# Seven block products in place of eight in a float32 feed-forward stage

## Chip, cores and metric

The kernel runs on one core of a Trainium2 chip. The metric is the device time of one execution in microseconds (us); lower is better. "Before" is the kernel as it was, "after" the changed one. A profiled execution gives a page (busy times, the chain of work that ended last, groups of instructions) and a trace that can be asked for single stretches of time. Engines are PE (TensorE), DVE (VectorE), ACT (ScalarE), POOL (GpSimd) and SP, which issues most DMAs.

## What is computed

A decoder of two layers, float32 throughout, for 8 sequences of 112 tokens and width 512: self-attention, cross-attention and feed-forward in each layer, each added to x. The change is in the last of them, layer 1's feed-forward, which works on the LayerNorm of x:

```python
def _L1_ffn_ref(x, w_gate, w_up, w_down):      # DIM_IN 512, DIM_HIDDEN 2048
    gate = jnp.einsum('bsd,hd->bsh', x, w_gate)
    up = jnp.einsum('bsd,hd->bsh', x, w_up)
    gated = jax.nn.silu(gate) * up
    return jnp.einsum('bsh,dh->bsd', gated, w_down)
...
x = x + _L1_ffn_ref(_layernorm(x, axis=-1), L1_ffn_w_gate, L1_ffn_w_up, L1_ffn_w_down)
```

## The kernel before

**Sizes.** There are NT = 896 tokens in NTT = 7 tiles of P = 128; HALF = 448 is half of the tokens, KC = 4 the number of blocks of 128 in the width of 512, NI = 256. x lies in SBUF as seven tiles `x[t]` of 128 tokens by 512.

**Stages.** The kernel runs one stage after another in one program. The changed stage, `l1_feed_forward` (line 1864), is the last. Before it, `l1_cross_attention` ends with a conditional part and, behind it, the output projections of the last two tiles (`project_out` on tiles 5 and 6, lines 1697 to 1701). After it, line 1891 stores the seven tiles of x, with one DMA of 256 KB each on SP's queue, in the order of tiles.

**The stage.** `layernorm_T` (line 247) normalises the seven tiles (VectorE, ScalarE for the root), transposes them on TensorE (line 235) and copies them on ScalarE (line 239) to `hT`, which holds the normalised tokens with the width on the partitions: 4 blocks of 128 by 896 tokens. The 2048 hidden units are 16 blocks of 128, in four weight tiles each of gate and up (`load_w`, line 155: 1 MB, four blocks of the width by 512 hidden units). For each block and each half of the tokens `gated` (line 1383) makes two products of four terms with `matmul_k` (line 257, its matmul at line 259), one into a bank of `mm_ps` and one into a bank of `sc_ps`: the weight block of 128x128 is stationary, 448 tokens move. ScalarE takes Silu of the gate's bank (line 1391), VectorE multiplies it by the up's bank (line 1392) into `h`, 16 blocks by 896 tokens. Then for each tile of tokens one product of 16 terms, with 128 tokens of `h` stationary and 512 columns of `wd` moving, goes into a bank of `tp_ps` (line 1878), and VectorE adds it to `x[t]` (line 1880).

**Buffers.** PSUM is eight banks of 128x512 float32 (`bank`, line 111), named by hand: `mm_ps` takes 0 and 1 in turn, `sc_ps` 2 and 3, `tp_ps` 4 and 5. The weight tiles rotate through the six buffers of the pool `wp` (line 94), so the load of the third down tile, for example, waits until the third gate tile has been read. A pool opened later takes SBUF that an earlier one has given back, and its first writes wait for the earlier one's last reads.

**Order.** In this stage no order is pinned by hand. When the program is built, each engine gets one queue, filled in the order in which the code is written, but work that is written later can be let ahead of work that is not yet ready. Within its queue an engine takes instructions strictly in turn. Semaphores are added where one engine needs another's result, or a buffer back.

A float32 matmul appears in the trace as two records of TensorE, each with its own weight load.

Of the kernel before, what the change touches and what calls it, by code (L numbers as in the profile page):

```python
# [21 lines left out]
FP = mybir.dt.float32  # L22
# [3 lines left out]
AF = mybir.ActivationFunctionType  # L26
ALU = mybir.AluOpType
# [3 lines left out]
P = 128  # L31
# [3 lines left out]
NTT = NT // P  # L35
HALF = NT // 2
# [6 lines left out]
NEXP, NI, TOPK = 32, 256, 8  # L43
# [15 lines left out]
def decoder(ctx: ExitStack, tc: tile.TileContext, a, out: bass.AP):  # L59
# [24 lines left out]
    V, A, G, T = (Engine(e) for e in (nc.vector, nc.scalar, nc.gpsimd, nc.tensor))  # L84
# [9 lines left out]
    wp = ctx.enter_context(tc.tile_pool(name="wp", bufs=6))  # L94
# [3 lines left out]
    work = [None]  # L98
    ps = ctx.enter_context(tc.tile_pool(name="ps", bufs=2, space=PSUM))

    @contextmanager
    def phase(name, waits="pool"):

        with tc.tile_pool(name=name, bufs=1, reuse_waits=waits) as stay, tc.tile_pool(
            name=f"{name}w", bufs=2, reuse_waits=waits
        ) as w:
            work[0] = w
            yield stay


    bank = [ps.tile([P, 512], FP, tag=f"bank{i}", name=f"bank{i}", bufs=1) for i in range(8)]
    turns = {"mm": 0, "sc": 0, "tp": 0}

    def turn(what):
        turns[what] += 1
        return turns[what] % 2

    def mm_ps():
        return bank[turn("mm")]

    def sc_ps():
        return bank[2 + turn("sc")]

    def tp_ps():
        return bank[4 + turn("tp")]
# [25 lines left out]
    x = [xp.tile([P, D], FP, tag=f"x{t}", name=f"x{t}") for t in range(NTT)]  # L151
# [3 lines left out]
    def load_w(src, name):  # L155
        w = wp.tile([P, 4, 512], FP, tag="w", name=name)
        nc.sync.dma_start(w, src)
        return w
# [88 lines left out]
    def layernorm_T(hT, root=rsqrt):  # L247
        for t in range(NTT):
            mvr = row_scales(x[t], root)
            xn = normed_rows()  # L250
            normed(xn, x[t], mvr)
            transpose_tile(hT, xn, t)

    def new_hT():
        return act.tile([P, KC, NT], FP, tag="hT", name="hT")

    def matmul_k(dst, lhs, rhs, n=KC):
        for k in range(n):
            T.matmul(dst, lhs(k), rhs(k), start=(k == 0), stop=(k == n - 1))  # L259
# [140 lines left out]
    def all_of(pieces):  # L400

        while True:
            try:
                next(pieces)
            except StopIteration as end:
                return end.value
# [106 lines left out]
    def any_early():  # L513

        with tc.tile_pool(name="early", bufs=1) as tmp:
            return counted_early(tmp)
# [863 lines left out]
                V.tensor_tensor(x[t], x[t], odd[:, t, :], ALU.add)  # L1380
            sort.close()

    def gated(dst, wg, wu, hT, halves=(0, 1)):

        for half in halves:
            tok = slice(half * HALF, (half + 1) * HALF)
            pg, pu = mm_ps(), sc_ps()
            matmul_k(pg[:, :HALF], lambda k: wg[:, k, :], lambda k: hT[:, k, tok])
            matmul_k(pu[:, :HALF], lambda k: wu[:, k, :], lambda k: hT[:, k, tok])
            sg = work[0].tile([P, HALF], FP, tag="sg", name="sg")  # L1390
            A.activation(sg, pg[:, :HALF], AF.Silu)
            V.tensor_tensor(dst[:, tok], sg, pu[:, :HALF], ALU.mult)  # L1392


    def l1_self_attention():
# [466 lines left out]


    def l1_feed_forward():
        with phase("f1") as p0:
            hT = new_hT()
            layernorm_T(hT)
            h = p0.tile([P, 16, NT], FP, tag="hid", name="hid")
            for i in range(4):
                wg, wu = load_w(a["f1_wg"][i], "f1_wg"), load_w(a["f1_wu"][i], "f1_wu")  # L1870
                for c in range(4):
                    cs = slice(c * P, (c + 1) * P)
                    gated(h[:, 4 * i + c, :], wg[:, :, cs], wu[:, :, cs], hT)
            wd = [load_w(a["f1_wd"][i], "f1_wd") for i in range(4)]
            for t in range(NTT):
                po = tp_ps()
                matmul_k(
                    po, lambda k: h[:, k, t * P : (t + 1) * P], lambda k: wd[k // 4][:, k % 4, :], 16
                )
                V.tensor_tensor(x[t], x[t], po, ALU.add)  # L1880

    early0, early1 = any_early()
    l0_self_attention()
    with tc.tile_pool(name="y", bufs=1) as yp:
        y_all = yp.tile([P, NTT, D], FP, tag="y", name="y")
        y = [y_all[:, t, :] for t in range(NTT)]
        l0_block(yp, y, *l0_cross_attention(early0, y))
    l1_cross_attention(early1, l1_self_attention())
    l1_feed_forward()
    for t in range(NTT):  # L1890
        nc.sync.dma_start(out[t * P : (t + 1) * P, :], x[t])
# [106 lines left out]
```

## Time and profile before

| what | us |
|---|---|
| median of 3 runs (lowest, highest) | 2064.79 (2064.42, 2069.33) |
| profiled execution, its time | 2061.26 |
| profiled execution, its span (first to last instruction) | 2059.5 |
| TensorE busy in the span | 1960.6 |
| first product of the changed stage starts at | 1765.10 |
| last product of the ups ends, products with `wd` begin at | 1959.2 |
| last add to x starts at | 2055.53 |
| mean granted TensorE clock over the span | 0.978 |

Times inside the profile count from the span's start. In the lists below, a line of the timeline reads: start, length, engine, line of the kernel, operation, what is written from what, shape, number of records merged, and in brackets how long the engine stood idle before and who released it. A group's line ends with busy time, the mean of one, idle time before its instructions and the releaser. A line of the chain has start, length, engine, tile and line. Line L80 is that of the helper that issues instructions where an order is pinned, so many operations of earlier stages share it. Records of matmuls overlap: the length of one is not the distance between two.

### The profile page before, as it was taken

The numbers are of one execution on the slowest core, as the hardware profiler recorded it, in microseconds if no ns is written. First come the engines' busy times: TensorE is split into PE (matmuls) and PEld (weight loads), VectorE is DVE, ScalarE is ACT, GpSimd is POOL, SyncE is SP. The second block draws the span as 40 slices with busy tenths as digits, with TensorE's granted clock in tenths as the row PEclk, the third lists the DMA queues.
The fourth block names the chain that finished last, engine by engine and source line by source line (L and its number), as shares of the span: only waits on it lengthen the run. The fifth ranks groups of instructions, "written<-read, shape, count | busy, mean of one in ns | idle before, by whom it ended". The sixth has DMA issues, their size and how long they took to land. (4 is left out here: it accounts for less than half of the span.)

```text
span 2059.5 us, 26414 instructions
## 1 busy us (share of the span) xinstructions
PE 1960.6 (95%) x10033; PEld 1172.4 (57%) x10033; DVE 905.4 (44%) x1929; ACT 561.7 (27%) x1316; POOL 609.0 (30%) x766
## 2 busy tenths in 40 slices
PE   8999989999999999988999999988899898999999
PEld 4545664455555555555778888854556454455544
DVE  4662556375666656645222222233776465310100
ACT  3543321021222212332111111121666465200000
POOL 2252032132222222222566666612554122000000
PEclk9999989999999999989999999999999999999999
DMA  4105010243334433446877677660011301011100
GB/s 175 42 22 171 13 42 32 77 143 116 133 125 134 148 115 120 155 146 249 244 188 187 159 180 183 129 166 24 22 37 36 94 22 63 22 41 41 41 16 21
DMA packets 82021, 209.62 MB, mean 102 GB/s; under 512 B 32979, under 2 KB 38227, under 8 KB 72788
## 3 DMA queue, kind: packets, MB, share of 16 engines
q1 hardware_dynamic: 57588, 134.27, 19.7%
q0 software_dynamic: 24288, 73.47, 14.0%
q8 instruction: 85, 1.39, 0.3%
q14 instruction: 60, 0.49, 0.1%
HBM read 245.31 MB, written 78.76 MB: 157 GB/s over the span
## 5 line engine op out<-in xcount | busy, mean ns | idle before, releaser
L259 PE MATMUL bank<-f_wo,oT 128*128 128x512 f32 x448 | 210.5, 594 | 0.0
L259 PE MATMUL bank<-hT,f_wq 128*128 128x448 f32 x512 | 202.6, 540 | 0.0
L80 PEld LDWEIGHTS bank<-hbT,wb 128*128 128x128 f32 x1408 | 164.0, 192 | 20.2 <-issue 20.2
L80 PE MATMUL bank<-hbT,wb 128*128 128x128 f32 x1408 | 164.3, 275 | 0.0
L80 DVE TENSOR_TENSOR hidb<-sgb,bank 128x256 f32<-128x256 f32 x66 | 27.8, 421 | 289.5 <-ACT sgb L80 289.5
L904 POOL TENSOR_TENSOR s<-s,rec 112x448 f32<-112x448 f32 x64 | 59.7, 933 | 322.3 <-ACT pT L306 258.2
L259 PEld LDWEIGHTS bank<-hT,f_wq 128*128 128x128 f32 x512 | 93.8, 190 | 78.2 <-issue 78.0
L80 POOL TENSOR_TENSOR st<-st,rec 112x448 f32<-112x448 f32 (+1 forms) x95 | 82.8, 903 | 146.0 <-DVE rec L80 80.9
L259 PEld LDWEIGHTS bank<-f_wo,oT 128*128 128x128 f32 x448 | 80.7, 190 | 76.0 <-issue 76.0
L80 POOL DMA_INDIRECT acc<-ob,row_out x66 | 106.3, 1610 | 35.2 <-issue 18.3
L80 ACT ACTIVATE st<-st,mxs 112x112 f32<-112x112 f32 (+1 forms) x383 | 111.0, 380 | 0.0
L298 ACT ACTIVATE s<-s 112x448 f32<-112x448 f32 x64 | 36.9, 577 | 243.9 <-DVE s L297 229.3
L259 PE MATMUL bank<-hT,f_wg 128*128 128x448 f32 x256 | 101.9, 539 | 0.0
L259 PE MATMUL bank<-hT,f_wu 128*128 128x448 f32 x256 | 101.4, 539 | 0.0
L259 PE MATMUL bank<-f_wd,hid 128*128 128x512 f32 x224 | 96.3, 592 | 0.0
L1392 DVE TENSOR_TENSOR hid<-sg,bank 128x448 f32<-128x448 f32 x32 | 19.9, 621 | 172.7 <-PE bank L259 172.7
L922 DVE TENSOR_TENSOR y<-y,bank 128x512 f32<-128x512 f32 x56 | 38.5, 687 | 124.6 <-PE bank L259 124.6
L848 POOL TENSOR_TENSOR qT<-qT,qs 128x448 f32<-128x448 f32 x64 | 72.3, 1130 | 63.4 <-DVE qs L844 63.4
L844 DVE TENSOR_TENSOR qs<-bank,shape_consts 64x448 f32<-64x448 f32 x144 | 89.5, 622 | 2.9
L80 PE MATMUL bank<-wb,hidb 128*128 128x512 f32 x176 | 84.0, 600 | 0.0
L80 ACT ACTIVATE sgb<-bank 128x256 f32<-128x256 f32 x66 | 25.4, 384 | 196.8 <-PE bank L80 196.8
L80 ACT ACTIVATE ob<-bank,pw 128x512 f32<-128x512 f32 x66 | 45.4, 687 | 122.3 <-PE bank L80 122.3
(363 smaller groups left out, 3417.3 us busy)
## 6 DMA issues: line engine op xcount, KB each, us to landing
weights<-in_e_wg SPq DMA_DIRECT2D x64, 256.0 KB
weights<-in_e_wu SPq DMA_DIRECT2D x64, 256.0 KB
weights<-in_e_wd SPq DMA_DIRECT2D x64, 256.0 KB
f_wq<-in_f_wq SPq DMA_DIRECT2D x8, 1024.0 KB
f_wo<-in_f_wo SPq DMA_DIRECT2D x8, 1024.0 KB
cTe<-in_ctxT SPq DMA_DIRECT2D x8, 558.0 KB
f_wg<-in_f_wg SPq DMA_DIRECT2D x4, 1024.0 KB
f_wu<-in_f_wu SPq DMA_DIRECT2D x4, 1024.0 KB
```

Source lines behind the costliest of these rows:

```text
L80: done = issue(*args, **kw)
L259: T.matmul(dst, lhs(k), rhs(k), start=(k == 0), stop=(k == n - 1))
L298: A.activation(s, s, AF.Exp)
L844: V.tensor_tensor(qs[lo : lo + 64], src[hi : hi + 64], sin0[lo : lo + 64].unsqueeze(1).to_broadcast([64, HB, S]), ALU.mult,)
L848: G.tensor_tensor(d, d, qs, ALU.add)
L904: G.tensor_tensor(s, s, rec.unsqueeze(2).to_broadcast([S, 4, S]), ALU.mult)
L922: V.tensor_tensor(y[t], y[t], project_rows(oT, wo, t), ALU.add)
L1392: V.tensor_tensor(dst[:, tok], sg, pu[:, :HALF], ALU.mult)
```

## The change

The two matrix products of the stage (tokens by gate and up weights, hidden units by down weights) are each cut into 2x2 blocks and computed with seven block products in the Strassen-Winograd form instead of eight.

For gates and ups, two hidden blocks of 128 are the rows, two halves of the width the inner index and two halves of the tokens the columns. Four sums of weight blocks (`row_sums`, on GpSimd, for each weight and each pair of hidden blocks) and four sums of token blocks (`column_sums`, on VectorE, once) are formed first. For the down product, two tiles of tokens are the rows, even and odd blocks of the hidden units the inner index, and two halves of 256 columns of `wd` the columns: four column sums of 128x8x256 on VectorE once, four row sums of 128x8x128 on GpSimd for each of three pairs of tiles. The seventh tile is computed as before, ahead of the pairs, into bank 6.

`seven_products` uses three banks a, b and c. Four products accumulate in a, and ScalarE copies a out after the first, the second and the third; two go into c, and VectorE reads c between them; one goes into b. Each of the four results is a bank's content plus, in three cases, one of the copies: for gates VectorE adds and ScalarE takes Silu, for ups VectorE adds and GpSimd multiplies (the fourth is multiplied on VectorE from the bank), for the down product GpSimd adds the copy to x and VectorE adds the bank. Gates use banks 0 to 2 and ups 3 to 5, as do even and odd pairs of tiles. `in_turn` interleaves the groups: first product of a group, then the rest of the group before it, then the middle of the group.

```diff
-    def gated(dst, wg, wu, hT, halves=(0, 1)):
-        for half in halves:
-            tok = slice(half * HALF, (half + 1) * HALF)
-            pg, pu = mm_ps(), sc_ps()
-            matmul_k(pg[:, :HALF], lambda k: wg[:, k, :], lambda k: hT[:, k, tok])
-            matmul_k(pu[:, :HALF], lambda k: wu[:, k, :], lambda k: hT[:, k, tok])
-            sg = work[0].tile([P, HALF], FP, tag="sg", name="sg")
-            A.activation(sg, pg[:, :HALF], AF.Silu)
-            V.tensor_tensor(dst[:, tok], sg, pu[:, :HALF], ALU.mult)
+    def row_sums(dst, top, bottom, eng):
+        eng.tensor_tensor(dst(0), bottom[0], bottom[1], ALU.add)
+        eng.tensor_tensor(dst(1), dst(0), top[0], ALU.subtract)
+        eng.tensor_tensor(dst(2), top[0], bottom[0], ALU.subtract)
+        eng.tensor_tensor(dst(3), top[1], dst(1), ALU.subtract)
+
+    def column_sums(dst, left, right, eng):
+        eng.tensor_tensor(dst(0), right[0], left[0], ALU.subtract)
+        eng.tensor_tensor(dst(1), right[1], dst(0), ALU.subtract)
+        eng.tensor_tensor(dst(2), right[1], right[0], ALU.subtract)
+        eng.tensor_tensor(dst(3), left[1], dst(1), ALU.subtract)
+
+    def seven_products(banks, n, terms, top, bottom, rows, left, right, columns, copies, take):
+        a, b, c = (bank[:, :n] for bank in banks)
+
+        def product(dst, lhs, rhs, first=False, part=None):
+            for k in range(terms) if part is None else part:
+                T.matmul(dst, lhs(k), rhs(k), start=first and k == 0, stop=k == terms - 1,
+                         skip_group_check=True)
+
+        def copied(i):
+            A.copy(copies[i], a)
+            return copies[i]
+
+        few = range(terms if terms < 4 else terms // 2)
+        product(a, top[0], left[0], first=True)
+        m1 = copied(0)
+        yield
+        product(c, rows[0], columns[0], first=True)
+        product(a, rows[1], columns[1])
+        u2 = copied(1)
+        product(b, top[1], left[1], first=True, part=few)
+        product(a, rows[2], columns[2])
+        u3 = copied(2)
+        yield
+        take(1, 1, c, u3)
+        product(b, top[1], left[1], part=range(len(few), terms))
+        take(0, 0, b, m1)
+        product(a, bottom[1], columns[3])
+        take(1, 0, a, None)
+        product(c, rows[3], right[1])
+        take(0, 1, c, u2)
+
+    def in_turn(products):
+        last = iter(())
+        for one in products:
+            next(one)
+            all_of(last)
+            next(one)
+            last = one
+        all_of(last)
...
     def l1_feed_forward():
...
-            for i in range(4):
-                wg, wu = load_w(a["f1_wg"][i], "f1_wg"), load_w(a["f1_wu"][i], "f1_wu")
-                for c in range(4):
-                    cs = slice(c * P, (c + 1) * P)
-                    gated(h[:, 4 * i + c, :], wg[:, :, cs], wu[:, :, cs], hT)
...
+                tokens = [gp.tile([P, 2, HALF], FP, tag=f"tok{i}", name=f"tok{i}") for i in range(4)]
+                for kk in range(2):
+                    column_sums(lambda i: tokens[i][:, kk, :],
+                                *([of_hT(k, half)(kk) for k in range(2)] for half in range(2)), V)
+
+                def projected(w, p, banks, take):
...
+                    sums = gp.tile([P, 4, 2, P], FP, tag="sums", name="sums", bufs=3)
+                    row_sums(lambda i: sums[:, i], *([block(m, k) for k in range(2)] for m in range(2)),
+                             G)
+                    copies = [gp.tile([P, HALF], FP, tag=f"copy{i}", name="copy", bufs=2)
+                              for i in range(3)]
+                    return seven_products(
+                        banks, HALF, 2, *([of(block(m, k)) for k in range(2)] for m in range(2)),
+                        [of(sums[:, i]) for i in range(4)],
+                        *([of_hT(k, half) for k in range(2)] for half in range(2)),
+                        [of(t) for t in tokens], copies, take,
+                    )
+
+                def gates_and_ups(wg, wu, p, dst):
+                    gates = {}
+
+                    def take_gate(m, half, pp, more):
+                        g = gates[m, half] = gp.tile([P, HALF], FP, tag="g", name="g", bufs=7)
+                        if more is not None:
+                            V.tensor_tensor(g, pp, more, ALU.add)
+                            pp = g
+                        A.activation(g, pp, AF.Silu)
+
+                    def take_up(m, half, pp, more):
+                        d = dst[:, m, half * HALF : (half + 1) * HALF]
+                        g = gates[m, half]
+                        if more is None:
+                            V.tensor_tensor(d, pp, g, ALU.mult)
+                        else:
+                            V.tensor_tensor(more, pp, more, ALU.add)
+                            G.tensor_tensor(d, more, g, ALU.mult)
+
+                    yield projected(wg, p, (bank[0], bank[1], bank[2]), take_gate)
+                    yield projected(wu, p, (bank[3], bank[4], bank[5]), take_up)
+
+                def all_gates_and_ups():
+                    for i in range(4):
+                        wg, wu = load_w(a["f1_wg"][i], "f1_wg"), load_w(a["f1_wu"][i], "f1_wu")
+                        for p in range(2):
+                            c = 4 * i + 2 * p
+                            yield from gates_and_ups(wg, wu, p, h[:, c : c + 2])
+
+                in_turn(all_gates_and_ups())
             wd = [load_w(a["f1_wd"][i], "f1_wd") for i in range(4)]
-            for t in range(NTT):
-                po = tp_ps()
-                matmul_k(
-                    po, lambda k: h[:, k, t * P : (t + 1) * P], lambda k: wd[k // 4][:, k % 4, :], 16
-                )
...
+                columns = [wp.tile([P, 8, NI], FP, tag="w", name="colsum") if i < 2 else
+                           dp.tile([P, 8, NI], FP, tag=f"colsum{i}", name="colsum") for i in range(4)]
+                for i in range(4):
+                    column_sums(lambda m: columns[m][:, 2 * i : 2 * i + 2],
+                                columns_of(i, 0), columns_of(i, 1), V)
+
+                t = NTT - 1
+                po = bank[6]
+                matmul_k(po, lambda k: h[:, k, t * P : (t + 1) * P],
+                         lambda k: wd[k // 4][:, k % 4, :], 16)
                 V.tensor_tensor(x[t], x[t], po, ALU.add)
+
+                def two_tiles(p):
+                    top, bottom = rows_of(2 * p), rows_of(2 * p + 1)
+                    rows = [dp.tile([P, 8, P], FP, tag=f"rowsum{i}", name="rowsum", bufs=2)
+                            for i in range(4)]
+                    row_sums(lambda i: rows[i], top, bottom, G)
+                    copies = [dp.tile([P, NI], FP, tag=f"ucopy{i}", name="ucopy", bufs=2)
+                              for i in range(3)]
+
+                    def take(m, n, pp, more):
+                        d = x[2 * p + m][:, n * NI : (n + 1) * NI]
+                        if more is not None:
+                            G.tensor_tensor(d, d, more, ALU.add)
+                        V.tensor_tensor(d, d, pp, ALU.add)
+
+                    return seven_products(
+                        bank[:3] if p % 2 == 0 else bank[3:6], NI, 8,
+                        [of(r) for r in top], [of(r) for r in bottom], [of(r) for r in rows],
+                        *([columns_by(k, n) for k in range(2)] for n in range(2)),
+                        [of(c) for c in columns], copies, take,
+                    )
+
+                in_turn(two_tiles(p) for p in range(NTT // 2))
```

More of the change, by code (lines that the diff above doesn't have):

```diff
@@ L1868, in l1_feed_forward, with of_hT @@
             h = p0.tile([P, 16, NT], FP, tag="hid", name="hid")
-            for i in range(4):
-                wg, wu = load_w(a["f1_wg"][i], "f1_wg"), load_w(a["f1_wu"][i], "f1_wu")
-                for c in range(4):
-                    cs = slice(c * P, (c + 1) * P)
-                    gated(h[:, 4 * i + c, :], wg[:, :, cs], wu[:, :, cs], hT)
-            wd = [load_w(a["f1_wd"][i], "f1_wd") for i in range(4)]
-            for t in range(NTT):
-                po = tp_ps()
-                matmul_k(
-                    po, lambda k: h[:, k, t * P : (t + 1) * P], lambda k: wd[k // 4][:, k % 4, :], 16
-                )
-                V.tensor_tensor(x[t], x[t], po, ALU.add)
+            def of_hT(k, half):
+                return lambda kk: hT[:, 2 * k + kk, half * HALF : (half + 1) * HALF]
@@ new lines, in of, with block @@
+            def of(block):
+                return lambda kk: block[:, kk, :]
+            with ExitStack() as pools:
+                gp = pools.enter_context(tc.tile_pool(name="gates", bufs=1))
+                tokens = [gp.tile([P, 2, HALF], FP, tag=f"tok{i}", name=f"tok{i}") for i in range(4)]
[3 more added lines that the diff above has]
+                def projected(w, p, banks, take):
+                    def block(m, k):
+                        c = (2 * p + m) * P
+                        return w[:, 2 * k : 2 * k + 2, c : c + P]
+                    sums = gp.tile([P, 4, 2, P], FP, tag="sums", name="sums", bufs=3)
[34 more added lines that the diff above has]
+                in_turn(all_gates_and_ups())
@@ new lines, in l1_feed_forward, with rows_of, columns_of, columns_by @@
+            wd = [load_w(a["f1_wd"][i], "f1_wd") for i in range(4)]
+            def rows_of(t):
+                return [h[:, k::2, t * P : (t + 1) * P] for k in range(2)]
+            def columns_of(i, n):
+                return [wd[i][:, k::2, n * NI : (n + 1) * NI] for k in range(2)]
+            def columns_by(k, n):
+                return lambda kk: wd[kk // 2][:, 2 * (kk % 2) + k, n * NI : (n + 1) * NI]
+            with tc.tile_pool(name="down", bufs=1) as dp:
+                columns = [wp.tile([P, 8, NI], FP, tag="w", name="colsum") if i < 2 else
[7 more added lines that the diff above has]
+                         lambda k: wd[k // 4][:, k % 4, :], 16)
+                V.tensor_tensor(x[t], x[t], po, ALU.add)
+                def two_tiles(p):
[17 more added lines that the diff above has]
+                in_turn(two_tiles(p) for p in range(NTT // 2))
```

## The prediction

> **What bounds the kernel now.** I read the page's busy line first, then the chain of work that ended last, then the timeline and the groups of the last 300 us, where the changed stage lies.
>
> ```profile
> PE 1960.6 (95%) x10033; PEld 1172.4 (57%) x10033; DVE 905.4 (44%) x1929; ACT 561.7 (27%) x1316; POOL 609.0 (30%) x766
> ...
> 1767.84 0.60 PE bank L235 x4
> 1768.44 287.07 PE bank L259 x732
> 2055.53 0.69 DVE x L1880
> ```
>
> The last three lines end the chain: after the last four transposes of the stage's LayerNorm, TensorE runs 287.07 us without a gap through the products of line 259; one VectorE add and the store follow. No wait stands in this stretch, so its length is matmuls times spacing. The timeline gives the spacings, which the means of 539 and 592 ns hide because matmuls overlap:
>
> ```profile
> 1956.19 3.17 PE L259 MATMUL bank<-hT,f_wu 128*128 128x448 f32 x8
> ...
> 2034.73 20.76 PE L259 MATMUL bank<-f_wd,hid 128*128 128x512 f32 x48
> ...
> 1461.75 1.89 PE L80 MATMUL bank<-a_wv,hT 128*112 128x256 f32 x8
> ```
>
> Take the last one's own duration from the stretch and divide by the others: (3.17 - 0.54)/7 = 0.376 us for 448 columns, (20.76 - 0.592)/47 = 0.429 us for 512, (1.89 - 0.379)/7 = 0.216 us for 256 (from another stage, its stationary operand 112 wide; 128x128 products with 128-wide ones stand 0.111 apart at 1313.10, so a weight load hides behind 256 columns too). All three are 0.84 us per 1000 columns: halving the width costs nothing. A float32 product is two matmul records, so the counts below are of records. Check: 508 x 0.376 + 224 x 0.429 = 287.1.
>
> The other engines are nearly idle there:
>
> ```profile
> L1392 DVE TENSOR_TENSOR hid<-sg,bank 128x448 f32<-128x448 f32 x32 | 19.9, 621 | 172.7 <-PE bank L259 172.7
> L1391 ACT ACTIVATE sg<-bank 128x448 f32<-128x448 f32 x32 | 17.5, 546 | 168.2 <-PE bank L259 168.2
> ```
>
> Each waits some 170 us for TensorE; GpSimd has nothing in the stage. The granted clock is 1.00 in every stretch from 1760 to 2050, so no throttle muddies the count.
>
> **What falls away.** Gates and ups: 16 hidden blocks x 2 halves x 2 weights x 4 terms x 2 records = 512. Now 8 pairs of blocks x 2 weights x 7 products x 2 terms x 2 = 448, same shape. 64 x 0.376 = **-24.1 us**. Down: 7 tiles x 16 x 2 = 224 x 0.429 = 96.1. Now one tile as before, 32 x 0.429 = 13.7, and 3 pairs x 7 products x 8 terms x 2 = 336 at 0.216 = 72.6, together 86.3: **-9.8 us**. There are more matmuls, but narrower ones.
>
> **What is added, and its cover.** Prices: a GpSimd add of two SBUF operands takes 1.13 us at 448 elements (line 848) and 1.27 at 512 (line 419), so 2.1 ns an element: 0.72 at 256, some 2.4 to 2.5 at 1024. VectorE: 0.62 at 448 and 0.42 at 256 from PSUM, 0.64 at 448 and 0.69 at 512 with two SBUF inputs (lines 297, 1380). ScalarE: copies 0.53 at 448, 0.38 at 256, Silu 0.55.
> Per gate-and-up pair TensorE works 56 x 0.376 = 21.1 us. GpSimd needs 8 x 0.72 + 3 x 1.13 = 9.2, ScalarE 6 x 0.53 + 4 x 0.55 = 5.4, VectorE 7 x 0.62 = 4.3. Per pair of token tiles TensorE has 112 x 0.216 = 24.2 us, GpSimd 4 x 2.5 + 3 x 0.72 = 12.2, the others under 2. None becomes the bound. The copies between Silus load no table anew: the trace shows sqrt at 1758.50, a copy at 1760.03 and sqrt at 1762.95 without a load.
>
> **New waits on TensorE** are what could cost. Bank a is copied twice while it grows; the next product into a must wait for that copy, and everything later in TensorE's queue stands behind it. In between lies the product into b, 4 x 0.376 = 1.5 us, against 0.53 for the copy and some 0.15 of hand-over (TensorE to ScalarE took 0.03 at 1938.35, back 0.1 at 1763.77). Bank c is read by VectorE before its last product: copy 0.53, add 0.62 and hand-overs, some 1.5 us, against 3.0 of the other group's first product and this group's product into a. In the down pairs the covers are 1.7 to 3.4 us against 0.4 (copy) and 1.6 (copy, GpSimd add, VectorE add). So **0** inside the groups; if the cover is gone, see the slower rival.
>
> **Start**: +1.0, between 0 and 6. Before, products on the first half of the tokens were already placed ahead of the last transposes (the trace has f_wg at 1765.10, tile 6's transposes at 1767.84), so later-written work is let ahead when ready. Only four products, a and b of the first gate and the first up, need no token sums: 16 x 0.376 = 6.0 us; a quarter fits before 1767.84 as now, the rest lasts from 1768.44 to 1772.9. The token sums need the last hT copy (ended 1769.06), then five VectorE adds for the first block: 3.2 us, 1772.3, or up to 1.8 later where GpSimd's first weight sums (8 x 0.72, free to run once the last x of the stage before is done at 1765.08) hold them up. If nothing is let ahead, TensorE idles from 1768.44 to 1774.1.
>
> **Hand-over to down**: +0.5, between 0 and 6. The seventh tile's 13.7 us and the first pair's first product, 3.4, cover 16 VectorE column sums (11.0 us) and 4 GpSimd row sums (10.0 us). Row sums begin some 2 us after the last up product (add, multiply on GpSimd). Side by side they fit into 17.1. One after the other, 21 us + 2, the product on the first row and column sum could be 6 late. The trace leans towards taking turns:
>
> ```profile
> 1723.90 3.18 POOL L80 TENSOR_TENSOR st<-st,rec 112x384 f32<-112x384 f32 x4 [9.98 <-DVE mbt L80]
> 1737.06 3.65 POOL L80 TENSOR_TENSOR st<-st,rec 112x384 f32<-112x384 f32 x4 [9.98 <-DVE rec L80]
> ...
> 1738.55 0.69 DVE L80 SCALAR_TENSOR_TENSOR x<-g,x 128x512 f32<-128x512 f32 x1
> ```
>
> The same four GpSimd operations take 3.18 us whenever VectorE has no operation with two SBUF inputs beside them, and 0.47 more in the one group that has. I take near the low end because the first product needs only the first of four row sums, and the first column sums can start as soon as the last gate weights are free, 7 products (10.5 us) earlier. The Trainium skill ("SBUF — State Buffer", section "Who interferes with whom") says that a VectorE instruction with two SBUF inputs and a GpSimd one that reads SBUF exclude each other for a whole instruction; by that rule the sum takes the upper ends, the first rival below. The trace agrees in kind: 0.47 us lost to an operation of 0.69.
>
> **End**: VectorE's last add 0.42 in place of 0.69; tile 4 is now finished last, and stores 5 and 6 may queue behind its store in SP's queue: 256 KB at the 333 GB/s of the last store is 0.8 us each, so 0 to 1.6. Taken: +0.5.
>
> **Sum**: -24.1 - 9.8 + 1.0 + 0.5 + 0.5 = **-31.9 us**. The profiled execution ran 2061.3 us with a span of 2059.5, which gives 2027.6 of span and 2029.4; the median of the runs shown is 3.5 higher, so 2064.8 - 31.9 = **2033**. All stalls at nothing would give 2031, and against the profiled execution 2027.
>
> **Rivals.**
> 1. The sums take turns and nothing is let ahead: start +6, hand-over +6, -33.9 + 12.5 = -21.4: 2043. For it: the 0.47 us; against: the hoisted f_wg.
> 2. Slower: the reads of growing banks are not covered, because on TensorE's queue the product after a read stands next to it. Where a copy stands between matmuls now, TensorE does idle:
>
> ```profile
> 1739.98 0.59 PE L80 MATMUL bank<-ident,st 112*96 112x112 f32 x4 [0.67 <-ACT pTt L80]
> ```
>
> Price per group: two copies at 0.8 and one VectorE add at 0.9 make 2.5 us in 16 gate and up groups (40), and 2.7 in 3 down pairs (8): -31.9 + 48 = +16, 2081. It decides from 31.9/19 = 1.7 us per group. Against it: every such product has one of another bank written before it, and two groups are interleaved.
> 3. Half of these waits are open, some 1.3 to 1.9 us a group: no change, 2059 to 2070.
>
> **Chances.** Forecast, with 2026 to 2040 as its own range, 0.64; first rival 0.18; no change 0.06; slower 0.12. A difference under 0.3% (6 us) can't be told from none here. So faster 0.82, same 0.06, slower 0.12. The range runs from all covers holding and a run like the profiled one, less 2, to the first rival with another 8 us of small waits: 2025 to 2052.
>
> **What would show it.** Gate and up matmuls 448 of 448 columns 0.376 apart, 336 of 256 columns 0.216 apart; TensorE idle under 3 us after 1768; the gap, if any, at the first product with token sums and about 14 to 17 us after the last up. Wrong, if TensorE idles before products into a or c with ScalarE or VectorE named as releaser, if the 256-column spacing exceeds 0.25, or if GpSimd's adds of 1024 elements take over 5 us and TensorE waits for them.

## The result, and the profile after

The changed kernel takes 2039.4 us in the median of 4 runs (2036.46 to 2041.57), beside 2065.03 for the kernel before in 4 runs of the same comparison: a ratio of 0.987, 95% interval 0.985 to 0.989: 25.6 us less, clear of no change. In a second comparison, repeated as an experiment below, it was 0.985 (0.982 to 0.988). The forecast was 2033, with 2025 to 2052 as its range.

The busy line of the changed kernel's page, and the end of its chain of work (start, length, engine, tile, line, number of records):

```profile
PE 1930.7 (95%) x10113; PEld 1187.9 (58%) x10113; DVE 956.7 (47%) x1983; ACT 589.5 (29%) x1373; POOL 723.2 (35%) x875
...
1777.57 0.64 PE bank L235 x4
1778.24 0.60 ACT hT L239
...
1778.91 0.96 DVE tok L1394
1779.87 1.07 DVE tok L1396
...
1785.26 159.90 PE bank L1410 x424
1945.16 0.86 PE bank L259 x2
1946.02 3.04 PE bank L1410 x8
1949.06 12.87 PE bank L259 x30
1961.93 72.53 PE bank L1410 x336
```

There are 80 matmul records more (10033 to 10113: 336 + 32 + 448 in place of 512 + 224) and 29.9 us less of busy TensorE. Where the chain had 287 us of line 259 it now has the gates and ups (line 1410, 432 records in 159.90 + 3.04 us, 0.377 each), the seventh tile (line 259, 32 records) and the three pairs of tiles (336 records in 72.53 us, 0.216 each). From 1785.26 on no wait stands in the chain. Before it there is a new stretch: the copy of the last hT and six VectorE token sums.

**Which length to compare.** In this pair of profiles the spans differ by 21.1 us (2059.5 and 2038.4), the stage itself by more. It begins later in the profile of the changed kernel: the last four LayerNorm transposes start at 1777.57, against 1767.84 before. All that every engine issues ahead of the stage is the same in both kernels, instruction for instruction. So the stage is measured by **T, from the start of the last four transposes of line 235 to the end of the span**: 2059.5 - 1767.84 = 291.7 before, 2038.4 - 1777.57 = 260.8 after, 30.9 us less. The expectations of the first four groups of experiments count instead from the stage's first product, which starts 2.7 to 2.8 us earlier in these two profiles; an expected 266 from there is taken as an expected 263.2 in T. (In the kernels below that hold TensorE to the order of the text from the first product on, that product starts 0.5 to 0.9 us after the last transposes do; for them too the expectation is compared with T + 2.8.)

### The profile page after: what moved, and what is told of

Its sections match the earlier page's. It is cut to its first block, busy times and chain, and to the rows that moved or that the text cites. A ratio compares the mean times of both kernels' runs of the same rounds, so it can differ in the third digit from the quotient of the medians.

```text
span 2038.4 us, 26870 instructions
## 1 busy us (share of the span) xinstructions
PE 1930.7 (95%) x10113; PEld 1187.9 (58%) x10113; DVE 956.7 (47%) x1983; ACT 589.5 (29%) x1373; POOL 723.2 (35%) x875
## 5 line engine op out<-in xcount | busy, mean ns | idle before, releaser
L80 POOL DMA_INDIRECT hrow<-hrows,row_in x66 | 63.9, 969 | 47.0 <-DVE free L80 23.2
L80 POOL DMA_INDIRECT wb<-weights,wrow x44 | 46.3, 1052 | 95.9 <-PE bank L80 74.1
L1410 PE MATMUL bank<-tok,sums 128*128 128x448 f32 x192 | 78.1, 541 | 2.0 <-DVE tok L1394 1.4
L888 PEld LDWEIGHTS bank<-kT,qT 128*112 128x112 f32 x512 | 59.6, 178 | 27.6 <-issue 25.6
```

The lines of the kernel that those rows point to most:

```text
L80: done = issue(*args, **kw)
L888: T.matmul(sc[:S, j * S : (j + 1) * S], qT[:, j, tok], kT[:, hg // 2, tok], start=True, stop=True,)
L1410: T.matmul(dst, lhs(k), rhs(k), start=first and k == 0, stop=k == terms - 1, skip_group_check=True)
```

## The experiments

### Both kernels again, and each half alone

Open after the first comparison: the stage had shortened by 30.9 us, the medians by 25.6. Either the stages ahead of it became slower through the change (systematic), or they vary from execution to execution with both kernels. Two of the four kernels are copies of the two compared; the other two take one half of the change each.

```diff
 # gates only: in l1_feed_forward, after's gates and ups, before's loop over tiles
...
-                in_turn(two_tiles(p) for p in range(NTT // 2))
+            for t in range(NTT):
+                po = tp_ps()
+                matmul_k(po, lambda k: h[:, k, t * P : (t + 1) * P], ..., 16)
+                V.tensor_tensor(x[t], x[t], po, ALU.add)
 # down only: before's gates and ups, after's down product
...
-                in_turn(all_gates_and_ups())
...
+                    gated(h[:, 4 * i + c, :], wg[:, :, cs], wu[:, :, cs], hT)
```

> The changed kernel once more. Theory V (the earlier stages vary from execution to execution, in both kernels alike): first product of the stage anywhere from 1764 to 1776 us, stage from there to the end again 263 to 265 us, and over more rounds the gain over the kernel before grows from 26 towards 31 us. Theory S (the change lengthens the earlier stages by some 5 us each time): first product at 1770 to 1776 in this profile too, gain stays at 25 to 27.

> The kernel before, once more, as a second sample of its earlier stages. Theory V: first product of the stage at 1764 to 1776 us, not always 1765. Theory S: at 1764 to 1768 again. Both: 294 to 295 us from there to the end, time within 0.2% of the kernel before.

> Seven products for gates and ups alone, down product as before. By the sum: stage shorter by 24.1 less some 2 of start, 272 to 273 us. Rival (the gain comes mostly from somewhere else): over 280.

> Seven products for the down product alone, gates and ups as before. By the sum: stage shorter by 9.8 plus or minus 1, 284 to 286 us, and TensorE without a gap at the hand-over. Rival (column and row sums that take turns hold up the first pair): 288 to 291 us, with a gap of 3 to 6 us behind the seventh tile.

| kernel | last transposes at | span | T | median of runs (lowest to highest, runs) | ratio to before, 95% |
|---|---|---|---|---|---|
| before | 1767.84 | 2059.5 | 291.7 | 2068.61 (2059.42 to 2077.01, 23) | |
| before again | 1773.85 | 2065.6 | 291.8 | 2066.58 (2061.05 to 2073.04, 10) | 0.9997 (0.9977 to 1.0017) |
| after again | 1779.39 | 2040.1 | 260.7 | 2036.87 (2031.50 to 2044.50, 6) | 0.9849 (0.9817 to 0.9881) |
| gates only | 1776.53 | 2047.3 | 270.8 | 2047.35 (2046.13 to 2052.99, 5) | 0.9905 (0.9874 to 0.9936) |
| down only | 1771.75 | 2053.4 | 281.7 | 2057.57 (2052.92 to 2065.82, 9) | 0.9948 (0.9925 to 0.9972) |

(The runs of before are those of this comparison, its profile the one shown at first.) T repeats within 0.1 us, the start of the stage does not: the copy of before begins it 6.0 us later than before did, and in the kernels with the new gates, these and the ones below, the last transposes start anywhere from 1769.20 to 1780.01. So the early stages vary from execution to execution, and a loss of 5 us each time is not borne out. With more runs the medians differ by 2068.61 - 2036.87 = 31.7 us, near the stage's gain of 30.9; but the interval of the ratio leaves 24.6 to 37.9 us, so a smaller systematic loss is not excluded. The start of the stage's first product in the copy of after, 1776.49, lies half a microsecond outside the ranges of both theories.

The halves add up: gates and ups 291.7 - 270.8 = 20.9, down 291.7 - 281.7 = 10.0, together 30.9. Down only is where it was expected; gates only is 273.6 in the expectation's counting, 0.6 above its 272 to 273. Their chains, gates only and then down only:

```profile
1784.16 159.90 PE bank L1410 x424
...
1947.95 95.29 PE bank L259 x222
```

```profile
1772.38 204.66 PE bank L259 x540
1977.04 72.53 PE bank L1422 x336
```

In the first, the old down product follows the new gates; in the second, 508 records of gates and ups and the seventh tile's 32 run as one stretch of line 259 straight after the transposes, with no token sums ahead of it. The start costs only where the new gates are.

### The order on TensorE: as written, group by group, and bare

The forecast costed the reads of growing banks at nothing because other products stand between a read and the next product into its bank. Three kernels keep TensorE's instructions in the order in which the text issues them and take that cover away in steps.

```diff
 # as written: TensorE alone keeps the order of the text in this stage
-            return partial(self.issue_next, issue) if Engine.pinned else issue
+            return partial(self.issue_next, issue) if self.pinned else issue
+                T.pinned = True
                 in_turn(all_gates_and_ups())
+                T.pinned = False
 # one by one: as written, and no group between another's parts
-                in_turn(all_gates_and_ups())
+                for one in all_gates_and_ups():
+                    all_of(one)
 # bare: one by one, and no other bank's product between a read and the next product into a bank
+            product(b, top[1], left[1], first=True)
+            product(a, top[0], left[0], first=True)
+            m1 = copied(0)
+            take(0, 0, b, m1)
...
+            product(a, rows[1], columns[1])
+            u2 = copied(1)
+            product(a, rows[2], columns[2])
+            u3 = copied(2)
...
+            product(c, rows[0], columns[0], first=True)
+            take(1, 1, c, u3)
+            product(c, rows[3], right[1])
```

> TensorE takes the gate and up products exactly in the order of the code, so nothing is let ahead at the start. If letting ahead is what covers the token sums: 10 of the first 16 records done when TensorE stops waiting, 6 x 0.376 = 2.3 us lost, stage 265.5 to 267 us against 263.7; the rest of the stage as before, since the code's order covers the reads. If the order that the build chooses matters all through the stage: over 270.

> The same, with the gate and up groups one after the other, not interleaved. By the covers: the copy before the product into a of bottom and the fourth column sum stands uncovered, 0.53 + 0.15, so 0.7 to 0.85 us per group, 16 groups, 11 to 13 us: stage 277 to 280 us. By the slower rival's price of 2.5 us per group: 304 to 308.

> The same seven products per group, but ordered so that both copies and the VectorE add stand between two products into the same bank, and groups not interleaved. The slower rival's place, made real: 2.5 us per group x 16 = 40 on top of 266, stage 302 to 310 us, slower than the kernel before (294.4). If TensorE rides over such reads (weights loaded ahead, short hand-overs): under 285.

T was **263.0** as written, **277.9** one by one and **315.3** bare, whole times 2041.42, 2052.72 and 2089.95 in one execution each (before: median 2069.06). As written is where it was expected. The other two are above: with the 2.8 us added they are 280.7 where 277 to 280 was expected, and 318.1 for 302 to 310.

Not all of this is order. From the last transposes to the last product the granted clock is 1.00 in the profiles of before, after, their copies and the two halves. In these three it drops to 0.50 for a while: from 1775.8 to 1779.2 as written, from 1778.0 to 1781.4 and 1979.4 to 1986.2 one by one, and from 1781.5 to 1788.3 and 2010.2 to 2023.8 bare. Records take twice as long there: six in 4.05 us one by one, which are 2.64 in the next list, and eight in 6.17 bare, which are 3.25 further down.

```profile
1778.34 4.05 PE L80 MATMUL bank<-tok,sums 128*128 128x448 f32 x6 [2.16 <-DVE tok L1394]
```

```profile
1782.41 6.17 PE L80 MATMUL bank<-tok,sums 128*128 128x448 f32 x8 [0.62 <-ACT copy L1414]
```

Bare, TensorE is busy for 12.1 us of the two stretches, so at most some 6 us of its T are the clock's (an estimate: half of that time).

As written, TensorE's only wait of over a microsecond in the stage is at the start (its timeline; the bracket is the idle time and its releaser):

```profile
1782.65 2.64 PE L80 MATMUL bank<-tok,sums 128*128 128x448 f32 x6 [2.00 <-DVE tok L1394]
```

So the cover inside the groups comes from the order of the text; what the queue rearranges is at the start, and worth at most 263.0 - 260.8 = 2.2 us. Some 0.5 of these are the clock: the last transposes take 1.09 us and not 0.63, and the first token sum starts 1.80 us after they do, where it is 1.34 in the changed kernel. That the 2.2 is near the 2.3 expected is therefore in part luck. One by one, the last product into a stands right behind the one before it and waits for the third copy (first two lines of its timeline); from the eighth group on the queue fills that gap with two records of the seventh tile (third line), and the fourth line is the price of that:

```profile
1786.01 1.77 PE L80 MATMUL bank<-tok,f_wg 128*128 128x448 f32 x4 [0.62 <-ACT copy L1414]
1797.42 1.77 PE L80 MATMUL bank<-tok,f_wu 128*128 128x448 f32 x4 [0.62 <-ACT copy L1414]
...
1865.28 1.02 PE L259 MATMUL bank<-f_wd,hid 128*128 128x512 f32 x2
...
1980.64 2.07 PE L1410 MATMUL bank<-colsum,rowsum 128*128 128x256 f32 x4 [4.28 <-DVE colsum L1395]
```

A group takes 11.41 us (from 1786.01 to 1797.42; 11.44 in the mean, to the sixteenth at 1957.66) where the kernel as written, which has no wait there, takes 10.52 (28 records, 0.3758 apart): 0.89 lost for 0.62 of idle time. The rest is that the record before the wait lasts 0.54 and not 0.376, and that the first records after it start 0.10 slower (1.77 for four, 1.67 elsewhere). 16 x 0.92 is 14.7, where T is 14.9 longer. What else differs cancels to within about a microsecond. The 18 records of the seventh tile that went into gaps gained nothing: 16 more than as written, 6.9 us, but then the tile is shorter where it covers the column sums, and TensorE loses 4.4 + 1.0 + 1.7 = 7.1 us there, between 1976 and 1986, by the distances of its stretches. Only the 4.4 is the wait; the 2.7 is the clock of 0.50, under which the four records of the fourth line take 2.07 us (1.03 elsewhere). With the 1.4 us that the six records above lose, the clock makes some 4 us of this kernel's T; without them it would be near the low end of what was expected.

Bare, the stalls of one group of an up and the next of a gate are:

```profile
1796.42 1.74 PE L80 MATMUL bank<-tok,sums 128*128 128x448 f32 x4 [0.71 <-ACT copy L1414]
1798.88 3.25 PE L80 MATMUL bank<-tok,sums 128*128 128x448 f32 x8 [0.71 <-ACT copy L1414]
1803.00 1.74 PE L80 MATMUL bank<-hT,sums 128*128 128x448 f32 x4 [0.88 <-DVE copy L1990]
...
1810.02 1.74 PE L80 MATMUL bank<-tok,sums 128*128 128x448 f32 x4 [0.77 <-ACT copy L1414]
```

Two copies and one VectorE add per group, as the slower rival has it; the distance from the first line to the last is 13.60, which is 3.08 more than 10.52 (0.71 + 0.88 + 0.77 = 2.36 idle, and 0.24 for each of the three restarts). The eight groups from 1806.08 on take 13.55 in the mean, 3.03 more, and 16 x 3.03 = 48.5 of the 52.3 over the kernel as written; the rest is a balance of the clock, of longer waits for the column sums (6.80 and 4.55 us) and of records of the seventh tile that fill gaps. This kernel's stage is 315.3 - 291.7 = 23.6 us **longer** than that of the kernel before, with the same seven products. The groups run at a clock of 1.00 from the second on, and what they lose alone is more than the 30.9 us of the saving: the saving rests on the cover.

### Products ahead of the token sums

```diff
 # start ahead: as written, with b of the first gate and up right behind a,
 # and the first up's a and b ahead of the first gate's other products
+        early = ahead.pop() if ahead else False
         product(a, top[0], left[0], first=True)
         m1 = copied(0)
+        if early:
+            product(b, top[1], left[1], first=True, part=few)
         yield
...
-        product(b, top[1], left[1], first=True, part=few)
+        if not early:
+            product(b, top[1], left[1], first=True, part=few)
...
+            if ahead:
+                started = next(products)
+                next(started)
             all_of(last)
...
 # the token sums by result, for both halves of the width at once
-                for kk in range(2):
-                    column_sums(lambda i: tokens[i][:, kk, :], ..., V)
+                for _ in zip(*both):
+                    pass
```

> As written, but the a and b products of the first gate and the first up come first, and the token sums are made block by block for both halves of the width. If the start's 2.7 us are the wait for token sums: 16 records after the last transposes, then no gap, stage 262 to 263 us. If something else holds the start: 264 or more, with TensorE waiting for token sums still.

T was **262.0** where 259.2 to 260.2 was expected (with the 2.8 us added 264.8 for 262 to 263): a miss, and worse than the changed kernel's 260.8. The waits for the token sums are gone from its timeline, but others stand in their place:

```profile
1785.42 1.77 PE L80 MATMUL bank<-tok,sums 128*128 128x448 f32 x4 [0.62 <-ACT copy L1422]
1787.81 1.77 PE L80 MATMUL bank<-tok,f_wg 128*128 128x448 f32 x4 [0.62 <-ACT copy L1422]
...
1794.81 1.74 PE L80 MATMUL bank<-tok,sums 128*128 128x448 f32 x4 [0.71 <-ACT copy L1422]
```

The products into b, and the next group's first product, that were moved ahead had been the cover between two products into a. It is the wait of the kernels above, met by accident: three times, 1.95 us idle and, at the 0.89 and more that one costs, the 2.8 us between 262.0 and the low end of what was expected. Its whole time was 2039.05 in one execution.

### The hand-over to the down product

The first rival's mechanism is that VectorE's and GpSimd's sums take turns. One kernel puts the row sums of the pairs on VectorE, so that nothing of GpSimd's runs beside the column sums; the other takes away the cover by moving the seventh tile behind the pairs.

```diff
 # row sums on VectorE
-                    row_sums(lambda i: rows[i], top, bottom, G)
+                    row_sums(lambda i: rows[i], top, bottom, V)
 # seventh tile last
-                t = NTT - 1
-                ...
-                V.tensor_tensor(x[t], x[t], po, ALU.add)
...
                 in_turn(two_tiles(p) for p in range(NTT // 2))
+                t = NTT - 1
+                ...
+                V.tensor_tensor(x[t], x[t], po, ALU.add)
```

> The down product's row sums on VectorE in place of GpSimd, so that GpSimd reads SBUF only for its few adds to x. If two SBUF inputs of VectorE and GpSimd's reads exclude each other: the column sums, 1.2 to 2.8 us each in the changed kernel, return to 0.69, and a row sum of 1024 takes 1.3 to 1.4. If they are slow for another reason (strides, buffers): they stay above 1.2. Stage in both cases 263 to 265 us, since TensorE did not wait for them.

> The seventh tile's product, 13.7 us, stands behind the pairs and covers nothing. If it is what hides the sums that take turns: TensorE waits for the second column sum until some 20 us after the last up product, where it could use it after 7, stage 272 to 276 us. If the sums ran side by side: 267 to 268. If they were never on the path: 264.

First the changed kernel's own timeline of GpSimd and VectorE at this place, put in order of time:

```profile
1954.42 2.79 POOL L1389 TENSOR_TENSOR rowsum<-hid 128x1024 f32<-128x1024 f32 x1
...
1954.94 2.83 DVE L1396 TENSOR_TENSOR colsum<-f_wd 128x512 f32<-128x512 f32 x1
...
1957.69 2.83 DVE L1397 TENSOR_TENSOR colsum<-f_wd,colsum 128x512 f32<-128x512 f32 x1
...
1965.22 7.07 PE L1410 MATMUL bank<-colsum,rowsum 128*128 128x256 f32 x32
```

One sum of each engine every 2.75 us: VectorE's, 0.68 to 0.69 alone, ends only when GpSimd's 2.79 has run beside it. TensorE's product with the first sums (last line) follows the seventh tile and the first product with no gap. The groups of the same sums, in the changed kernel and then with the row sums on VectorE (busy time, mean ns of one, idle time before):

```profile
L1397 DVE TENSOR_TENSOR colsum<-f_wd,colsum 128x512 f32<-128x512 f32 x4 | 11.3, 2834 | 0.0
L1387 POOL TENSOR_TENSOR rowsum<-hid 128x1024 f32<-128x1024 f32 x3 | 8.0, 2666 | 0.1
```

```profile
L1397 DVE TENSOR_TENSOR colsum<-f_wd,colsum 128x512 f32<-128x512 f32 x4 | 2.7, 684 | 0.0
L1387 DVE TENSOR_TENSOR rowsum<-hid 128x1024 f32<-128x1024 f32 x3 | 3.7, 1220 | 2.1 <-PE bank L1410 2.1
```

The column sum goes from 2834 back to 684 ns when GpSimd is quiet, and the row sum is 1220 ns on VectorE (1.3 to 1.4 us expected). Yet T is **260.9** against 260.8 (whole time 2036.98 in one execution): a fourfold price, off the path. With the seventh tile last, T is **273.9** (276.8 from the first product, 0.8 above the 272 to 276 expected; whole time 2044.97), and TensorE's timeline shows what the tile had covered:

```profile
1946.16 8.37 PE L1410 MATMUL bank<-colsum,rowsum 128*128 128x256 f32 x28 [2.87 <-POOL rowsum L1387]
1960.47 2.07 PE L1410 MATMUL bank<-colsum,rowsum 128*128 128x256 f32 x4 [5.94 <-DVE colsum L1395]
```

Two waits of 8.8 us together; T is 13.1 longer in all. The clock explains most of the rest: it is 0.50 from 1946.5 to 1949.9, inside the 28 records that take 8.37 us where 28 x 0.216 is 6.05, and from 1956.8 to 1963.6, where the four records of the second line take 2.07 (1.03 at 1936.64 of the same trace). TensorE works for some 6.5 us of these stretches, so some 3.3 us are the clock's (an estimate: half of that time), and without them the kernel would lie in the expected range. About 1 us stays open.

### The start, with the cover kept

From the first miss follows what a better start needs: the first gate's and first up's products woven so that both hold, four products ahead of the token sums and never two products in a row into a bank that is being read.

```diff
+        if ahead:
+            ahead.pop()
+            product(a, top[0], left[0], first=True)
+            m1 = copied(0)
+            T.pinned = True
+            product(b, top[1], left[1], first=True)
+            yield
+            product(c, rows[0], columns[0], first=True)
+            yield
...
-                in_turn(all_gates_and_ups())
+                groups = all_gates_and_ups()
+                g0, u0 = next(groups), next(groups)
+                for one in (g0, u0, g0, g0, u0, g0, u0, g0, u0):
+                    next(one)
+                all_of(g0)
+                in_turn(groups, u0)
+                T.pinned = False
```

In it, a group's first step is its products into a and b, the second the first product into c, the third and fourth the next two into a, the fifth the results and the last product into a. The token sums go by result, as in the miss above.

> The a and b products of the first gate and up first, then these two groups woven so that another product stands behind every copied one; token sums block by block for both halves of the width. If the start's 2.7 us are the wait for token sums, and e3_start_ahead only exchanged it for three uncovered copies: TensorE without a gap after the last transposes, from their start to the end 258 to 259 us against 260.8. If the gap moves again to another sum or copy: 260 or more. The time over the rounds cannot tell 2.7 us from none.

T was **258.0** (expected 258 to 259), 2.8 us less than the changed kernel. TensorE's timeline behind its last transposes, which start at 1780.01 here:

```profile
1781.98 3.17 PE L80 MATMUL bank<-hT,f_wu 128*128 128x448 f32 x8
1784.99 7.68 PE L80 MATMUL bank<-tok,sums 128*128 128x448 f32 x20
```

Eight records of the up, and then products with sums, without a gap, at a clock of 1.00. In 4 runs the median was 2031.89 (2029.87 to 2040.0), a ratio of 0.981 (0.977 to 0.986) to before, 2066.98 in the 7 runs beside it. These runs can't tell the last 2.8 us from the changed kernel's 2036.87; that they are saved is shown by the stage in the profile alone.

## Why the prediction was right, step by step

**Gates and ups, -24.1.** Behind the first 16 records on either side, 432 records took 162.94 us, 0.377 each, and the other 496 of before took 186.4 (from 1772.79 to 1959.20), 0.376 each. That is -23.5. Right, but for a thousandth of a microsecond per record.

**Down, -9.8.** Seventh tile 0.86 + 12.87 = 13.73, pairs 72.53, together 86.26, against 96.30 in the profile before: -10.0. Right, and the halving of the width cost nothing, as counted from another stage's 112-wide products.

**Inside the groups, 0.** Right, and the reason is shown: as written, with nothing let ahead, the groups still follow each other 10.52 us apart, and when the cover goes, waits for the copies and for VectorE appear at the places that the second rival named. Its price of 2.5 us per group was too low: 3.03 in the mean, since each wait costs its restart too. The cover is worth 16 x 3.03 = 48.5 us in this stage; the T of 263.0 against 315.3 holds some clock besides.

**Start, +1.0. This step was mis-sized: +2.8.** The seventeenth record started 7.69 us after the stage's first product before (at 1772.79), and 10.52 after (at 1785.26). The expectations' 2.7 took the end of the sixteenth record before, 7.85. The step counted on four products, 16 records, to run ahead of the first token sum. In the trace:

```profile
1779.97 0.99 PE L1410 MATMUL bank<-tok,sums 128*128 128x448 f32 x2 [0.27 <-issue]
1780.80 0.92 PE L1410 MATMUL bank<-hT,f_wu 128*128 128x448 f32 x2
1783.13 1.77 PE L1410 MATMUL bank<-tok,sums 128*128 128x448 f32 x4 [1.42 <-DVE tok L1394]
1785.26 1.02 PE L1410 MATMUL bank<-tok,sums 128*128 128x448 f32 x2 [0.36 <-DVE tok L1395]
```

Only 8 records of the first gate and 2 of the up ran ahead; the first term of the product into c, which needs only sums over the first half of the width, was put before most of the up's products, and the second term then stood at the head of the queue for 1.42 us. And the sums were late: VectorE's took 1.07 us each (start to start, in the chain) in place of the 0.64 of the prediction's row, beside GpSimd's weight sums at 1.11 in place of 0.72:

```profile
1778.67 0.72 POOL L1388 TENSOR_TENSOR sums<-sums,f_wu 128x256 f32<-128x256 f32 x1
1779.35 1.10 POOL L1389 TENSOR_TENSOR sums<-f_wu 128x256 f32<-128x256 f32 x1
```

This is GpSimd's timeline; its adds lengthen at 1779.35, when VectorE has begun its first token sum (1778.91). The prediction had allowed for this with "up to 1.8 later", and its range of 0 to 6 held it. In the kernel with the start covered the sums are as slow (each pair of them takes 2.0 to 2.2 us), and it gets the 2.8 back whole (258.0 in T for 260.8): the loss was one of order, of the products and of the sums.

**Hand-over to down, +0.5, and the end, +0.5. Both were 0.** The sums take turns, as the first rival said and as the Trainium skill has it ("SBUF — State Buffer", section "Who interferes with whom": the two exclude each other for a whole instruction); this trace agrees, with 2834 ns against 684. But it decided nothing, since the first column sums were done at 1940.8, before the last up product, as argued, and the last part of the second ones at 1968.8, some 2.5 us before the product that begins at 1968.67 reaches its last quarter (12 x 0.216 later). With the seventh tile's cover gone it does decide, with waits of 8.8 us. From the last product's end to the end of the span it is 3.9 us (4.0 before).

**The sum.** -23.5 - 10.0 + 2.8 = -30.7 for -31.9 forecast. The profiles gave 294.4 - 263.7 = 30.7 from the stage's first product (1765.10 and 1774.74), 30.9 in T. The mechanism was right; that the sum came within 1.2 us is in part luck, since the start was 1.8 dearer than its term and the hand-over and the end 1.0 cheaper. The medians differ by 25.6 in the first comparison and by 31.7 in the longer one. The forecast of 2033 started from a median of three runs at 2064.8, and the runs of the changed kernel then came out at 2039.4 and 2036.87. That distance is not a step of the sum: it lies ahead of the stage, where executions of one kernel differ by as much; a small loss there through the change is not excluded.

## What to carry to other kernels

Where a chain shows one engine without a wait, count its instructions times their spacing: each removed term here paid within 3% what the row said, whether a product was dropped or made narrower. Seven products pay only if each bank that is read while it grows has another bank's product between the read and its next product; the same arithmetic in a bare order made the stage 23.6 us longer than eight products. When work is moved ahead to fill one gap, look at what it had been covering where it stood. Before the difference of two stretches is put down to an order or a wait, compare the granted clock in both.

## What was not expected of the hardware

**Turns between VectorE and GpSimd can cost one of them far more than the other.** Two VectorE adds of 0.64 and 0.69 us became 1.07 and 2.75, each time the length of GpSimd's add beside it, while GpSimd's went from 0.72 to 1.11 and from 2.35 to 2.79.

**A short wait of TensorE costs more than its idle time**: 0.89 us for 0.62 idle, 3.08 for three waits with 2.36, at a granted clock of 1.00.

**Half clock stands beside the longer waits.** The stretches at a clock of 0.50 in the stage are some 3.4, 6.8 or 13.6 us long, and each begins within or right behind a wait of TensorE of 2.1 to 6.8 us. They occur only in four kernels that were made to wait. Not every such wait has one: the kernel with products ahead of the token sums waits 2.31 us before its last transposes and has a clock of 1.00 from there on. That the waits cause them is not shown by a run of its own.

**The whole time and the granted clock move together.** Over the 23 runs of the kernel before, the span and the mean granted clock correlate with -0.90, some 2.1 us per 0.001: 2075.3 us at 0.972, 2057.7 to 2057.9 at 0.978 to 0.979. These 17.6 us are more than half of this change's gain, and enough to let four runs of each miss it by 6 us. T differs by 0.1 us between the two profiles of before, whose spans differ by 6.1, so there the variation lies ahead of the stage. Which of the two drives the other, the clock or the waits, is not shown.
